# Attention and mixture-of-experts block on one Trainium2 core: value products, projections, transposes and filler units in another order on TensorE

## The chip, the core and the metric

The kernel runs on one core of one Trainium2 chip. The metric is device microseconds of one execution, from start to end. The engines are named as in the profile: PE (TensorE, matrix products; PEld is its weight loads), DVE (VectorE), ACT (ScalarE), POOL (GpSimd) and SP (SyncE, which issues most DMA transfers). Each has a queue of its own and works through it in order; they wait for each other by semaphores.

## The reference, cut to what matters

One sequence of 2048 tokens with 128 features goes through causal attention (16 heads of 64) and then a mixture of 8 experts (2 chosen for each token) with one shared expert. All is float32.

```python
x = x + attn(layernorm(x))            # 16 heads, D = 64, causal, softmax over keys
#   qkv    = x @ qkv_w + qkv_b
#   probs  = softmax(where(mask, q @ k.T / 8, -0.7 * float32_max))
#   result = (probs @ v) @ out_w + out_b
x = x + shared_ffn(layernorm(x)) + sum over the 2 best experts of weight * expert_ffn(layernorm(x))
#   ffn(x) = (silu(x @ gate.T) * (x @ up.T)) @ down.T      # 352 hidden features
```

## The kernel before, in words

**Steps.** The 16 heads are taken as 8 pairs j, the 2048 tokens as 16 blocks of 128, and the blocks of queries as 8 pairs m, each with the keys of blocks 0 to 2m+1. A step is one (j, m); there are 64. Within a pair the order of m is `turns = [2, 7, 0, 6, 1, 5, 3, 4]` (L393), so that a short step (m = 2, 0, 1, 3) and a long one (m = 7, 6, 5, 4) take turns. `at` is the place in the pair, 0 to 7; m=2 has `at` 0 and six key blocks.

**Scores.** `score_units` (L403) gives units that each compute one 512-wide piece of scores for both heads on PE (L438, form 64*128 of the array), which DVE scales, masks and copies out of PSUM with a row maximum (L449, L453). After the last piece of a row ACT takes the exponential (L470). The scores of a step are computed four steps ahead if it is long, two if it is short (`coming`, L701).

**Transposes.** The probabilities must be turned before the product with the values. Of a short step all blocks are turned on PE (`turn`, L532, matmul L538) and copied out of PSUM by ACT to `pT` (L541). Of a long step most blocks go another way: DVE transposes 32x32 squares (L512), and DMA moves them to DRAM and back (`stage`, L516, then `turned`, L530). The two or four blocks on and next to the diagonal, the tail, are turned on PE and copied by ACT to `tail` (`turn_last`, L543), two steps ahead.

**Values and projection.** `times_v` (L563) multiplies by the values (L570, form 128*64 of the array) and adds up in one of two PSUM buffers `av`. After the last block, `divide` (L589) multiplies by the inverse sums on DVE, which gives `aT`. `finish` (L672) calls `project` (L594): two products with the output weights on PE (L597, form 128*128) and one addition into the residual `xr` on DVE (L598). It is called one group after the division; until then the step stands in `ending`. In the last pair it also starts the routing of finished tokens (`route_units`, L214), whose units `route_on` (L664) runs one at a time.

**PSUM.** Scores, transposes, projections and q/k/v units take their PSUM tiles from one pool of six buffers in turn (`psp`, L161, tag "r"). A matmul that opens a tile waits until the tile six places back has been copied out by DVE or ACT.

**Filler.** `fill` holds the q, k and v units of the next pair (L361, L378); DVE copies out q (L371), ACT k (L373) and v (L385).

**Order.** For PE and DVE the order of the program is the order of the queue (`manual_schedule`, L630); on ACT, POOL and SP the framework's scheduler sets it. The loop over the steps (L681) runs two or three groups of each step. A long step (`near` is true) has three: the tail (k = 0), and two halves of the blocks that came by DMA (k = 1, 2). In each group the loop does, in this order: one filler unit (short steps), transposes that are due on DVE, the turns of the group's blocks on PE, `finish` of the step before if one stands in `ending`, the products with the values, `divide`, one filler unit (long steps), in a long step's k = 0 the tails of the step after next, in k = 1 the load of `turned`, and then three units of scores. In the second group of a long step PE therefore has the projection of the short step before, then the values of the first half:

```python
            if ending is not None:
                finish(*ending)
                ending = None
            ...
            for t in ready:
                jt, mt, b = t[:3]
                times_v(*t, qkv[jt][0][2])
```

**After attention** come the routing of the last tokens, a scatter of the tokens to their experts by POOL (L328), and the experts, whose results POOL scatters back (L991).

Of the kernel before, what the change touches and what calls it, by code (L numbers as in the profile page):

```python
# [23 lines left out]
def attention_then_moe(  # L24
# [58 lines left out]
    def load_wq(j, engine):  # L83
        wq_of[j] = norm.tile([P, 3, 2, D], F32, tag="wq", name=f"wq_{j}", bufs=3)
        engine.dma_start(wq_of[j], qkv_w[:, :, 2 * j : 2 * j + 2, :])
# [7 lines left out]
    with nc.allow_non_contiguous_dma(reason="1024 numbers"):  # L93
# [16 lines left out]
        fill=MASKED,  # L110
# [6 lines left out]
    for e in range(NE):  # L117
# [9 lines left out]
        fill=0.0,  # L127
# [226 lines left out]
    def qkv_units(j):  # L354
        kT = pool.tile([P, S], F32, tag="kT", name=f"kT_{j}")
        qT = [None] * NG
        vt = pool.tile([P, NT, P], F32, tag="vt", name=f"vt_{j}")

        def qk_unit(s, n):
            pq = psp.tile([P, 512], F32, tag="r", name=f"pq_{j}_{s}_{n}")  # L360
            nc.tensor.matmul(  # L361
                pq,
                wq_of[j][:, s, :, :],
                xnT[:, ts(n, 512)],
                start=True,
                stop=True,
            )
            bias = bqk[:, s, j : j + 1]
            if s == 0:
                qT[n] = pool.tile([P, 512], F32, tag=f"qT{n}", name=f"qT_{j}_{n}", bufs=1)  # L370
                nc.vector.tensor_scalar_add(qT[n], pq, bias)  # L371
            else:
                nc.scalar.activation(kT[:, ts(n, 512)], pq, AF.Identity, bias=bias)  # L373

        def v_unit(g):
            pv = psp.tile([P, 4, P], F32, tag="r", name=f"pv_{j}_{g}")
            for t in range(4):
                nc.tensor.matmul(  # L378
                    pv[:, t, :],
                    xnT[:, ts(4 * g + t, P)],  # L380
                    wq_of[j][:, 2, :, :],
                    start=True,
                    stop=True,
                )
            nc.scalar.copy(vt[:, ts(g, 4), :], pv)  # L385

        q, k = ([lambda s=s, n=n: qk_unit(s, n) for n in range(NG)] for s in range(2))
        return (kT, qT, vt), q, k, [lambda g=g: v_unit(g) for g in range(NG)]
# [10 lines left out]
    def by_slabs(m):  # L399

        return (2 * m) // 4 * 4 if 2 * m >= NT // 2 else 0
# [130 lines left out]
    def turn(j, m, b, dst):  # L532

        tr = psp.tile([P, 2, 256], F32, tag="r", name=f"tr_{j}_{m}_{b}")
        q0 = 1 if b == 2 * m + 1 else 0
        for h in range(2):
            for q in range(q0, 2):
                nc.tensor.transpose(  # L538
                    tr[:, h, ts(q, P)], rows_of[j, m][q][:, h, ts(b, P)], ident
                )  # L540
        nc.scalar.copy(dst[:, :, q0 * P :], tr[:, :, q0 * P :])  # L541

    def turn_last(j, m):  # L543

        tail_of[j, m] = pool.tile([P, 4, 2, 256], F32, tag="tail", name=f"tail_{j}_{m}", bufs=1)
        for b in range(by_slabs(m), 2 * m + 2):
            turn(j, m, b, tail_of[j, m][:, b - by_slabs(m)])
# [41 lines left out]
    def divide(j, m):  # L589
        aT = pool.tile([P, 256], F32, tag="aT", name=f"aT_{j}_{m}", bufs=1)  # L590
        nc.vector.tensor_mul(aT, av_of[j, m], inb_of[j, m])
        return aT

    def project(j, m, aT):  # L594
        po = psp.tile([P, 2, E], F32, tag="r", name=f"po_{j}_{m}")
        for q in range(2):
            nc.tensor.matmul(po[:, q, :], aT[:, ts(q, P)], wo[:, j, :], start=True, stop=True)  # L597
        nc.vector.tensor_add(xr[:, ts(m, 2), :], xr[:, ts(m, 2), :], po)  # L598
# [22 lines left out]
    steps = [(j, m) for j in range(NP) for m in turns]  # L621
# [21 lines left out]
    fill, later = deque(), deque()  # L643
    last = []
    ending = None
# [3 lines left out]
    def load_shared():  # L649
        for k, w in enumerate((w_gate, w_up, w_down)):  # L650
            t = norm.tile([P, 3 * P], F32, tag="wq", name=f"shared_{k}", bufs=3)
            if k < 2:
                t = t[:, :F]
                nc.sync.dma_start(t, w[:, NE, :])
            else:
                t = t.rearrange("p (c e) -> p c e", c=NFC)
                for c, (f0, fn) in enumerate(FCH):
                    nc.sync.dma_start(t[:fn, c, :], w[f0 : f0 + fn, NE, :])
            shared_w.append(t)
# [4 lines left out]
    def route_on():  # L664

        for units in routes:
            u = units.popleft()
            if u:
                u()
        routes[:] = [units for units in routes if units]  # L670

    def finish(j, m, aT):  # L672
        project(j, m, aT)
        if j == NP - 1:
            for number, batch in enumerate(batches):
                if m == batch[-1]:
                    assert len(routes) <= 1
                    blocks = [b for m in batch for b in (2 * m, 2 * m + 1)]
                    routes.append(deque(route_units(blocks, number)))

    for n, (j, m) in enumerate(steps):  # L681
        at = n % NM
        if at == 0 and j + 1 < NP:
            qkv[j + 1] = qkv_units(j + 1)


            _, q, k, v = qkv[j + 1]
            fill.extend([*k, *v, q[3]])
            later.extend([q[1], q[0], q[2]])
            if j + 2 < NP:  # L690
                load_wq(j + 2, nc.sync)
        if at == 0 and j == NP - 1:
            load_shared()
        if at == 5 and later:
            assert not fill
            fill.extend(later)
            later.clear()
        if at == 6 and j + 1 < NP:
            assert not fill
        near = by_slabs(m)  # L700
        coming = scores_of(n + (4 if near else 2))  # L701
        if n == 0:
            coming.extend(scores_of(3))

        if near:
            groups = [list(range(near, 2 * m + 2))]
            groups += [list(range(k, k + near // 2)) for k in range(0, near, near // 2)]

            runs = [3, 3, len(coming) - 6] if n > 1 else [0, 3, 3]
        else:  # L710
            groups = [list(range(k, min(k + 3, 2 * m + 2))) for k in range(0, 2 * m + 2, 3)]
            half = len(coming) // 2 if n else 6
            runs = {1: [len(coming)], 2: [2 * (half // 2), half], 3: [0, half, half]}[len(groups)]
        for k, group in enumerate(groups):
            for _ in range(1 if n else 3):
                if fill and not near:
                    fill.popleft()()
            if n == 2:
                turn_slabs(2, age=False)
            turn_slabs(1)  # L720
            now = [turned(j, m, b) for b in group]
            if k == 0:
                spread(j, m)
            if ending is not None:
                finish(*ending)
                ending = None
            if n >= len(steps) - 2 and (n < len(steps) - 1 or k < 2):
                route_on()
            ready, last = (last + now, []) if near else (last, now)
            for t in ready:  # L730
                jt, mt, b = t[:3]
                times_v(*t, qkv[jt][0][2])
                if b == (by_slabs(mt) or 2 * mt + 2) - 1:
                    assert ending is None
                    ending = (jt, mt, divide(jt, mt))
            if n < len(steps) - 2:
                route_on()

            for _ in range(1 if n > 1 or k == 2 else 2):
                if fill and near:  # L740
                    fill.popleft()()
            if n < 2 and k == 1 - n:
                turn_slabs(2, age=False)
            turn_slabs(1, age=False, due=True)
            if n >= len(steps) - 2:
                route_on()
            if near and k == 0 and n + 2 < len(steps):
                turn_last(*steps[n + 2])
            if n == 0 and k == 0:
                turn_last(*steps[1])  # L750
                load_turned(*steps[1])
            if near and k == 1 and n + 2 < len(steps):
                load_turned(*steps[n + 2])
            for _ in range(runs[k] if k < len(groups) - 1 else len(coming)):
                if coming:
                    coming.popleft()()
            if len(steps) - 4 <= n < len(steps) - 2:
                route_on()
# [328 lines left out]
```

## Time and profile before

| | us |
|---|---|
| median of 3 runs | 1003.43 (1003.37 to 1006.6) |
| profiled execution | 1008.16, its span 1006.3 |
| PE busy | 943.7 (94%) |
| DVE busy | 749.7 (75%) |
| ACT busy | 540.9 (54%) |
| POOL busy | 204.9 (20%) |
| one head pair in the steady part, 400.40 to 500.64 | 100.24, of which PE is busy 98.09 |

In lines of the profile the columns of an instruction in order of time are: start in us from the span's start, busy us, engine, line of the kernel, operation, output <- input, shape, count, and in brackets how long the engine stood before it and what ended that wait. Rows of the same kind that follow each other are merged. In a table by stretch of time the columns are: stretch, its length, busy us and count of PE, PEld, DVE, ACT and POOL, the granted clock of PE (1.00 is full), the DMA engines' share and GB/s. In a list of waits they are: us in total, times, longest. Matmuls are pipelined and their ends are modelled, so an idle PEld does not mean that PE stands. A busy share is a mean over stages with different limits.

### The profile page before, as it was taken

How to read it: one execution, taken by the hardware profiler on the slowest of the kernel's cores; microseconds unless marked ns; L12 is line 12 of the kernel's file. 1: busy time of each engine (PE TensorE's matmuls, PEld its weight loads, DVE VectorE, ACT ScalarE, POOL GpSimd, SP SyncE). 2: the span in 40 equal slices, each digit the busy share in tenths (PEclk: the TensorE clock that was granted, in tenths of full speed). 3: DMA queues.
4: the chain of work that ended last, by engine and by line, in shares of the span. 5: the costliest groups of instructions: out<-in, count | busy, mean ns of one | idle time of the engine just before them, and what ended most of it. 6: DMA issues, size and time to landing. Idle time of an engine off the chain costs nothing. (4 is left out here: it accounts for less than half of the span.)

```text
span 1006.3 us, 18409 instructions
## 1 busy us (share of the span) xinstructions
PE 943.7 (94%) x5930; PEld 567.9 (56%) x5930; DVE 749.7 (75%) x2359; ACT 540.9 (54%) x1017; POOL 204.9 (20%) x393
## 2 busy tenths in 40 slices
PE   4998899999999999999999999999999898989996
PEld 1464555565556555655565556555655455657774
DVE  3786788778877877787778777877788886755554
ACT  4573556555655565556555655565466553425552
POOL 2040111111111111111111111111211103634441
PEclk9998999999999999999999999999999997999998
DMA  9568648864896488748874887588648864723104
GB/s 329 173 203 288 198 149 267 261 220 155 261 276 206 155 260 265 216 157 261 270 210 157 260 266 210 164 256 270 209 150 274 268 193 146 216 61 85 40 24 132
DMA packets 112670, 205.31 MB, mean 204 GB/s; under 512 B 16864, under 2 KB 104258, under 8 KB 107456
## 3 DMA queue, kind: packets, MB, share of 16 engines
q1 hardware_dynamic: 102816, 190.65, 59.4%
q0 software_dynamic: 8032, 13.22, 5.5%
q8 instruction: 48, 0.79, 0.3%
q10 hardware_dynamic: 1728, 0.27, 0.2%
q14 instruction: 46, 0.38, 0.1%
HBM read 105.10 MB, written 99.35 MB: 203 GB/s over the span
## 5 line engine op out<-in xcount | busy, mean ns | idle before, releaser
L470 ACT ACTIVATE row<-row,neg 128x1920 f32<-128x1920 f32 (+15 forms) x256 | 306.2, 1202 | 198.7 <-DVE neg L467 87.3
L438 PE MATMUL sc<-kT,qT 64*128 64x512 f32 (+3 forms) x1280 | 298.0, 552 | 11.3 <-ACT tail L541 5.2
L449 DVE TENSOR_SCALAR_CACHE_REDUCE row<-sc 128x512 f32<-128x512 f32 x384 | 243.3, 685 | 76.4 <-PE sc L438 65.8
L438 PEld LDWEIGHTS sc<-kT,qT 64*128 64x128 f32 x1280 | 123.9, 186 | 152.5 <-issue 83.6
L512 DVE STREAM_TRANSPOSE row<-row 128x1024 f32<-128x1024 f32 (+1 forms) x128 | 190.3, 1491 | 5.1 <-ACT row L470 5.1
L570 PE MATMUL av<-turned,vt 128*64 128x256 f32 x1280 | 158.3, 395 | 2.1 <-DMA turned<-stage 2.1
L453 DVE CUSTOM_DVE_ANT_0 row<-sc,mask 128x384 f32<-128x384 f32 (+3 forms) x256 | 114.9, 486 | 18.2 <-PE sc L438 17.6
L538 PE MATMUL tr<-ident,row 128*128 128x128 f32 x896 | 121.4, 281 | 6.5 <-DVE row L449 2.1
L538 PEld LDWEIGHTS tr<-ident,row 128*128 128x128 f32 x896 | 102.2, 144 | 41.1 <-issue 19.4
L570 PEld LDWEIGHTS av<-turned,vt 128*64 128x64 f32 x1280 | 88.5, 140 | 64.9 <-issue 23.5
L501 POOL DMA_DIRECT2D invd<-inv x60 | 43.1, 718 | 392.1 <-DVE inv L499 285.1
L541 ACT COPY pT<-tr 128x512 f32<-128x512 f32 (+1 forms) x160 | 78.6, 553 | 77.6 <-PE tr L538 77.2
L583 POOL DMA_DIRECT2D inb<-invd x120 | 71.6, 602 | 187.8 <-DMA invd<-inv 112.7
L570 PE MATMUL av<-pT,vt 128*64 128x256 f32 (+1 forms) x640 | 79.6, 371 | 6.3 <-ACT pT L541 5.9
L361 PE MATMUL pq<-xnT,wq 128*128 128x512 f32 x128 | 71.3, 647 | 0.1
L570 PEld LDWEIGHTS av<-pT,vt 128*64 128x64 f32 x640 | 38.5, 136 | 46.9 <-ACT pT L541 18.8
L541 ACT COPY tail<-tr 128x512 f32<-128x512 f32 x96 | 43.9, 520 | 15.1 <-PE tr L538 15.1
L991 POOL DMA_INDIRECT ybuf<-yo,to x39 | 38.3, 982 | 61.3 <-ACT yo L990 61.3
L371 DVE TENSOR_SCALAR qT<-pq,bqk 128x512 f32<-128x512 f32 x32 | 23.9, 747 | 34.6 <-PE pq L361 34.6
L470 ACT ACTIVATION_READ_ACCUMULATOR row<-row,neg 128x1 f32 x256 | 49.6, 194 | 0.0
L597 PE MATMUL po<-wo,aT 128*128 128x128 f32 x256 | 43.7, 294 | 5.7 <-DVE rest L280 2.5
L597 PEld LDWEIGHTS po<-wo,aT 128*128 128x128 f32 x256 | 34.0, 193 | 22.9 <-DVE row L449 16.3
(170 smaller groups left out, 894.8 us busy)
## 6 DMA issues: line engine op xcount, KB each, us to landing
stage<-row SPq DMA_DIRECT2D x256, 192.0 KB, 3.7
turned<-stage SPq DMA_DIRECT2D x16, 3072.0 KB, 11.1
stage<-row SPq DMA_DIRECT2D x256, 128.0 KB, 2.7
turned<-stage SPq DMA_DIRECT2D x16, 2048.0 KB, 8.7
zbuf<-zeros SPq DMA_DIRECT2D x8, 1056.0 KB, 11.4
inb<-invd POOLq DMA_DIRECT2D x120, 64.0 KB, 3.2
zs<-zbuf SPq DMA_DIRECT2D x39, 66.0 KB, 1.8
yt<-ybuf SPq DMA_DIRECT2D x4, 512.0 KB, 4.2
```

What stands on the lines that cost most here:

```text
L361: nc.tensor.matmul(pq, wq_of[j][:, s, :, :], xnT[:, ts(n, 512)], start=True, stop=True,)
L438: nc.tensor.matmul(sc[:, :cw], qT[i // 4][hd, ts(i % 4, P)], keys, start=True, stop=True)
L449: nc.vector.tensor_scalar(dst, src, SCALE, None, ALU.mult, ALU.max, accum_out=mh)
L453: nc.vector.tensor_tensor_reduce(out=rows[:, h, c0 : c0 + cw], in0=scs[h][:, :cw], in1=mask[:, 512 - cw : 512], scale=SCALE, scalar=-F32_M ...
L470: nc.scalar.activation(row, row, AF.Exp, bias=neg[:, h : h + 1], accum_out=sums[:, h : h + 1])
L501: small_dma(j, m)(invd_of[j, m].rearrange("n (a i) -> a n i", a=4), inv,)
L512: nc.vector.transpose(row, row)
L538: nc.tensor.transpose(tr[:, h, ts(q, P)], rows_of[j, m][q][:, h, ts(b, P)], ident)
L541: nc.scalar.copy(dst[:, :, q0 * P :], tr[:, :, q0 * P :])
L570: nc.tensor.matmul(av_of[j, m][hd, q0 * P :], vt[:, b, hd], pT[:, h], start=(b == near), stop=(b == (near or 2 * m + 2) - 1),)
L583: small_dma(j, m)(inb[h * D : (h + 1) * D, :].rearrange("d (q p) -> d q p", q=2), row.partition_broadcast(D),)
L597: nc.tensor.matmul(po[:, q, :], aT[:, ts(q, P)], wo[:, j, :], start=True, stop=True)
```

## The change

No instruction is added or taken away. The loop over the steps is edited in three places.

1. In a long step's second group (`near and k == 1`), `finish` is called behind the products with the values, not ahead of them. The projection's two matmuls come behind the first half's 8 or 12 blocks of values for both heads; then come the filler unit, if there is one, and the scores.
2. In a long step's first group, `turn_last` for the step after next is called ahead of the filler unit, not behind it. Step n = 1 keeps the old place.
3. In the second group of the six-block step (m = 2, `at` 0, from the second pair on), the filler unit comes behind the turns of the group's blocks and the projection, and ahead of the values; before, it came ahead of the turns.

In the built program DVE's order differs in one place: in the last pair, the addition of one projection (m = 3) into `xr` (L598) stands behind the routing's choice of the second expert instead of inside it. POOL's and SP's orders are the same. On ACT the copies follow: in m = 7's step the tail's copies stand ahead of a key copy, and the next key copy stands ahead of row 10's exponentials; in m = 6's the tail's copies stand ahead of a value copy; in m = 5's the first of the two tail copies stands ahead of row 7's exponentials, the second behind them, as before; in m = 2's a key copy stands behind the `pT` copies.

```diff
         for k, group in enumerate(groups):
             for _ in range(1 if n else 3):
-                if fill and not near:
+                if fill and not near and (at or not k or not n):
                     fill.popleft()()
...
             if k == 0:
                 spread(j, m)
-            if ending is not None:
+            values_first = near and k == 1
+            if ending is not None and not values_first:
                 finish(*ending)
                 ending = None
             if n >= len(steps) - 2 and (n < len(steps) - 1 or k < 2):
                 route_on()
+            if n and not at and k and fill:
+                fill.popleft()()
             ready, last = (last + now, []) if near else (last, now)
             for t in ready:
                 ...
                     ending = (jt, mt, divide(jt, mt))
+            if ending is not None and values_first:
+                finish(*ending)
+                ending = None
             if n < len(steps) - 2:
                 route_on()
+            if n > 1 and near and k == 0 and n + 2 < len(steps):
+                turn_last(*steps[n + 2])
 
             for _ in range(1 if n > 1 or k == 2 else 2):
                 if fill and near:
                     fill.popleft()()
...
-            if near and k == 0 and n + 2 < len(steps):
+            if n == 1 and k == 0:
                 turn_last(*steps[n + 2])
```

## The prediction, made before the changed kernel ran

> **What bounds the kernel now.** I read the page first, then the busy time of one head pair, then TensorE in order of time, and last the chain of waits at the end.
>
> ```profile
> span 1006.3 us, 18409 instructions
> PE 943.7 (94%) x5930; PEld 567.9 (56%) x5930; DVE 749.7 (75%) x2359; ACT 540.9 (54%) x1017; POOL 204.9 (20%) x393
> ```
>
> ```profile
> 400.40:500.64 100.24, 98.09 (x640) 56.40 (x640) 80.22 (x237) 57.87 (x106) 16.11 (x32) 1.00 0.72 225
> 832.30:845.80 13.50, 12.81 (x57) 8.81 (x58) 7.50 (x47) 2.52 (x8) 2.89 (x3) 0.50 0.60 206
> ```
>
> One head pair (eight steps) takes 100.24 us and repeats to the hundredth; PE is busy for 98.09 of it, DVE for 80.22, ACT for 57.87. So in the steady part only a few us a pair can be won, and only from PE. The second stretch is at the end of attention: PE ran at half its clock (the column that reads 0.50).
>
> The list of waits would have it that the projection is a place where PE stands:
>
> ```profile
> PEld po L597 <- DVE row L449: 16.3, 22, 1.5
> ```
>
> In order of time this is not so. The weight load idles while PE still streams scores:
>
> ```profile
> 405.53 2.21 PE L438 MATMUL sc<-kT,qT 64*128 64x512 f32 x12
> 407.67 0.71 PE L597 MATMUL po<-wo,aT 128*128 128x128 f32 x4
> 408.31 2.81 PE L570 MATMUL av<-turned,vt 128*64 128x256 f32 x24
> ...
> 427.36 1.13 PE L361 MATMUL pq<-xnT,wq 128*128 128x512 f32 x2
> 428.32 0.82 PE L538 MATMUL tr<-ident,row 128*128 128x128 f32 x6
> 429.07 2.59 PE L438 MATMUL sc<-kT,qT 64*128 64x512 f32 x8
> 432.27 1.40 PE L438 MATMUL sc<-kT,qT 64*128 64x512 f32 x4 [0.62 <-ACT tail L541]
> 433.60 0.71 PE L597 MATMUL po<-wo,aT 128*128 128x128 f32 x4
> ...
> 472.02 0.61 PE L597 MATMUL po<-wo,aT 128*128 128x128 f32 x4
> 472.46 1.02 PE L361 MATMUL pq<-xnT,wq 128*128 128x512 f32 x2
> 473.33 1.25 PE L538 MATMUL tr<-ident,row 128*128 128x128 f32 x10
> ```
>
> The reader is to see two things. First, the stall of a pair in step m=5: scores start at 429.07 and wait until 432.27 for ACT's copy of the tail, which stands in ACT's queue behind two exponentials:
>
> ```profile
> 429.38 1.15 ACT L470 ACTIVATE row<-row,neg 128x1024 f32<-128x1024 f32 x1 [3.02 <-DVE neg L467]
> 430.53 1.13 ACT L470 ACTIVATE row<-row,neg 128x1024 f32<-128x1024 f32 x1
> 431.66 0.83 ACT L541 COPY tail<-tr 128x512 f32<-128x512 f32 x2
> ```
>
> Second, a change of array form (the 64*128 of scores, the 128*64 of values, the 128*128 of the rest) costs PE time: the projection takes 0.64 between scores and values (407.67 to 408.31), but 0.44 between two 128*128 neighbours (472.02 to 472.46).
>
> At the end the chain goes through PE:
>
> ```profile
> 829.38 1.06 PE L260 MATMUL pr<-gwT,xnT 128*128 128x8 f32 x8
> 832.99 1.19 PE L597 MATMUL po<-wo,aT 128*128 128x128 f32 x4 [2.55 <-DVE rest L280]
> 834.11 3.68 PE L570 MATMUL av<-turned,vt 128*64 128x256 f32 x16
> 837.72 0.65 PE L301 MATMUL rk<-hot,below 128*128 128x40 f32 x2
> 839.96 3.68 PE L570 MATMUL av<-turned,vt 128*64 128x256 f32 x16
> ```
>
> The projection stands for 2.55 us behind DVE's routing, and the values behind it, which need nothing of that, take 3.68 instead of the 1.95 of the same row at 462.36.
>
> **The change part by part.** It adds and removes no instruction. POOL and SP keep their order, every DMA with them; DVE moves one addition, in the last pair; ACT follows PE's new order in copies.
>
> *Values ahead of the projection (long steps, second group).* In steady steps no wait goes, since none was there; what goes is a change of form where a 128*128 unit follows the values. Before: projection 0.64, then the q/k unit 1.05 (488.73 to 489.78), 1.69 together. After: the projection loses its way out (0.10) and the unit its way in (0.10; 0.96 at 427.36 against 0.87 at 472.46): 0.20 less. This holds for m=7, 6, 5 of pairs 1 to 6 and m=7, 5 of pair 0: 20 x 0.20 = -4.0. In m=4 scores follow, and three changes stay three: 0. In the first long step the values wait 2.1 for their transfer (78.88); the projection, 0.6, ran inside that wait and now comes behind it: +0.6. DVE's addition into xr waits for the later projection, and DVE's queue stands meanwhile. Behind it are q copies and evictions of scores that come after the projection on PE anyway, and DVE idled there 2.6, 2.55, 1.9 and 1.3 us (m=7, 6, 5, 4) against a delay of about 2.7, 2.7, 1.9 and 1.2 us: 0, with bounds of 0 and +0.4 for m=4, where it is closest. The values start 0.64 earlier; their transfers land some 7.5 to 11 us after issue, issued 18 us or more ahead (490.29 for 508.54): 0.
>
> *Tails' turns ahead of the filler.* In m=5 the turns run at 427.36, ACT idles from 426.4 and copies the first tail at once; the second copy (0.40) stays behind the exponentials, which DVE sets, and ends at about 432.05. The sixth score matrix alone now waits for it, and runs alone: 1.05 as in m=4 (460.67 to 461.72), so scores end at 433.2, not 433.60: -0.40 in seven pairs = -2.8. Bounds: 0 if the order on ACT costs as much again, -1.9 if the stall went whole. In m=7 and m=6 nothing stalled: 0. ACT now has the last key projection of m=7 ahead of row 10's exponentials, which end at about 493.3, not 490.6; DVE needs them at 495.76: 0, covered by 2.5 us.
>
> *A unit between turns and values (six-block step).* The values wait 0.98 for ACT's second copy at 475.52, behind row 13's exponentials. PE has the same work ahead of that point in either order: 0, bounds -0.1 and +0.1 a pair.
>
> *The last pair.* In m=6 the projection begins 1.02 after the last score matmul (806.06 to 807.08), against 0.20 in an earlier pair (407.46 to 407.67): -0.8. In m=7 it stood 0.9, but evictions then wait for staging transfers until 790.33: 0. In m=4 DVE's addition leaves the routing's chain: -0.3. In m=5 the first values run in the 2.55 us gap, at full clock 1.95; ranks then start at 834.4 (DVE's hot ends at 834.3) instead of 837.72, second values end at 837.6, and the next projection is free when DVE's chain reaches it at 840.1, not 846.70: -6.6 if the half clock goes with the gap. If it stays, ranks still start 3 us earlier: -3.0.
>
> [...] The rows first: the granted clock is 1.00 up to 832.2, 0.50 from 832.3 to 845.8 and 1.00 from 846.0, and the gap of 2.55 ends at 832.99. [...]
>
> **Sum.** -4.0 + 0.6 - 2.8 - 0.8 - 0.3 - 6.6 = -13.9, or -10.3 with the half clock kept. The profiled execution took 1008.16 us (span 1006.30, 1.86 around it), so 994.3; it lies 4.73 above the median, 1003.43. Half-clocked stretches may be part of that excess, so that the median has less of the last term to lose. From the median: 989.5 to 993.1. I take 991.
>
> **Rivals.** (1) The half clock stays or moves: 1003.43 - 10.3 = 993. For it: it lasted over 13.5 us though PE worked after 833. Against: another half-clocked stretch (0.50 from 801.6 to 804.8) also follows a gap of about 2 us, which ends at 801.49. [...] (2) The steady gain reappears as waits for evictions: DVE is busy 14.76 of the 15.49 us from 417.35 to 432.84. Then 6.2 of the sum goes and 4.1 to 7.7 stay: 996 to 999. Against: each such stretch begins with DVE idle for PE. (3) Slower: row 10's exponentials, 2.6 us late on ACT, make DVE's transposition and the staging behind it late. It decides once the delay passes the 2.5 us of cover; paid whole in seven pairs it is 18, less 10: 1011. Against: the cover is measured, and repeats. (4) Nothing is gained anywhere, as the projection wasn't waited for: 1003; against it speaks the 2.55 us gap.
>
> **How the numbers follow.** Forecast 0.52; half clock kept 0.20; (2) 0.16; (3) 0.06; (4) 0.06. 0.5% of 1003.43 is 5.0 us, about what a measurement of this kernel can tell from no change. Faster: 0.52 + 0.20 + half of (2), 0.08 = 0.80; same: 0.08 + 0.06 = 0.14; slower 0.06. The range reaches from the forecast with the tail stall gone whole (991 less 5) to the upper end of (2), 999.
>
> **What would show it.** A pair takes 99.2 us instead of 100.24; PE's wait for the tail's copy stays, on one score matrix; the projection follows the values at the same pitch; the slices at 832 lose their half clock, and row 10's exponentials start near 490.3 in that pair. I am wrong if the pair is longer, or if a longer wait for turned, vt or pT appears.

## The result, and the profile after

The changed kernel takes 993.31 us (median of 4 runs, 991.6 to 995.36), beside 1003.4 for the kernel before in the same comparison: a ratio of 0.9891, 95% interval 0.9867 to 0.9915. Its profiled execution took 992.08 us. The forecast was 991, the range 986 to 999.

The head of the page after (each engine's count is as before; the 6 records more are semaphore waits on PE):

```profile
span 990.2 us, 18415 instructions
PE 932.6 (94%) x5930; PEld 557.8 (56%) x5930; DVE 752.7 (76%) x2359; ACT 541.0 (55%) x1017; POOL 205.0 (21%) x393
```

One head pair, and a stretch at the end of attention that answers to the half-clocked one of before (columns as in the table by stretch of time: stretch, length, busy us and count of PE, PEld, DVE, ACT, POOL, granted clock, DMA share, GB/s):

```profile
396.58:495.60 99.02, 97.32 (x641) 55.67 (x640) 80.63 (x237) 57.94 (x105) 16.13 (x32) 1.00 0.73 227
...
828.00:841.00 13.00, 11.40 (x95) 8.31 (x96) 8.61 (x55) 5.67 (x15) 9.95 (x11) 1.00 0.47 172
```

A pair takes 99.02 us instead of 100.24, again to the hundredth in the steady part. PE's busy time in it falls by 0.77, its idle time by 0.45, so the gain is partly shorter work and partly a shorter stall. The granted clock is 1.00 all through that end stretch.

TensorE in order of time, after; step m=6, then m=5:

```profile
400.60 2.21 PE L438 MATMUL sc<-kT,qT 64*128 64x512 f32 x12
402.74 2.81 PE L570 MATMUL av<-turned,vt 128*64 128x256 f32 x24
405.48 0.71 PE L597 MATMUL po<-wo,aT 128*128 128x128 f32 x4
406.03 1.06 PE L378 MATMUL pv<-wq,xnT 128*128 128x128 f32 x8
407.02 2.42 PE L438 MATMUL sc<-kT,qT 64*128 64x512 f32 x12
...
422.31 0.88 PE L538 MATMUL tr<-ident,row 128*128 128x128 f32 x6
423.02 1.02 PE L361 MATMUL pq<-xnT,wq 128*128 128x512 f32 x2
423.97 2.84 PE L438 MATMUL sc<-kT,qT 64*128 64x512 f32 x10
426.98 1.12 PE L438 MATMUL sc<-kT,qT 64*128 64x512 f32 x2 [0.17 <-ACT tail L541]
```

The projection now takes 0.55 (405.48 to 406.03) instead of 0.64, and the v unit behind it 0.99 (406.03 to 407.02) instead of 1.09. In m=5 five of the six score matrices run through, and the sixth alone waits for ACT's second tail copy. ACT, around the same place:

```profile
423.05 0.58 ACT L541 COPY tail<-tr 128x512 f32<-128x512 f32 x1 [1.78 <-PE tr L538]
424.30 1.15 ACT L470 ACTIVATE row<-row,neg 128x1024 f32<-128x1024 f32 x1 [0.66 <-DVE neg L467]
...
425.45 1.13 ACT L470 ACTIVATE row<-row,neg 128x1024 f32<-128x1024 f32 x1
...
426.58 0.35 ACT L541 COPY tail<-tr 128x256 f32<-128x256 f32 x1
```

One copy stands ahead of row 7's exponentials, the other behind them. In the list of waits, the row that seemed to accuse the projection has shrunk from 16.3 to 0.8, and DVE's wait for the projection has grown from 18.8 to 51.7:

```profile
DVE xr L598 <- PE po L597: 51.7, 43, 6.9
...
PEld po L597 <- DVE row L449: 0.8, 2, 0.4
```

Neither number is a gain or a loss in itself: in e8 below the first row stays as long and the pair gets shorter, and e1, whose list has 52.4 for the second, has no longer step in its steady pairs. TensorE at the end of attention, in order of time:

```profile
819.36 1.95 PE L570 MATMUL av<-turned,vt 128*64 128x256 f32 x16
821.98 0.68 PE L597 MATMUL po<-wo,aT 128*128 128x128 f32 x4 [0.67 <-DVE rest L280]
823.42 0.39 PE L301 MATMUL rk<-hot,below 128*128 128x40 f32 x2 [0.76 <-DVE inv L496]
823.63 1.04 PE L309 MATMUL rk<-hot,ones 128*128 128x32 f32 x8
824.60 1.95 PE L570 MATMUL av<-turned,vt 128*64 128x256 f32 x16
```

The values run while DVE routes; the projection's wait is 0.67, where it was 2.55, and both halves of the values take 1.95, where they took 3.68.

Where the time went, by comparing the start of each step's first value product in the two traces: 1.87 us of the difference lie ahead of anything that the change touches (the start of the kernel); pair 0 gains 0.23; pairs 1 to 6 gain 1.22 each; the last pair gains 0.76 in m=7, 0.82 in m=6, 5.79 in m=5, 0.44 in the step after it and 0.25 in m=4; 1.4 are given back in the experts' part, behind the last projection.

### The profile page after: what moved, and what is told of

It is laid out like the page before. It is cut to its first block, busy times and chain, and to the rows that moved or that the text cites. A ratio compares the mean times of both kernels' runs of the same rounds, so it can differ in the third digit from the quotient of the medians.

```text
span 990.2 us, 18415 instructions
## 1 busy us (share of the span) xinstructions
PE 932.6 (94%) x5930; PEld 557.8 (56%) x5930; DVE 752.7 (76%) x2359; ACT 541.0 (55%) x1017; POOL 205.0 (21%) x393
## 5 line engine op out<-in xcount | busy, mean ns | idle before, releaser
L570 PE MATMUL av<-turned,vt 128*64 128x256 f32 x1280 | 154.8, 389 | 2.1 <-DMA turned<-stage 2.1
L538 PEld LDWEIGHTS tr<-ident,row 128*128 128x128 f32 x896 | 98.0, 141 | 34.5 <-DVE row L449 13.4
L361 PE MATMUL pq<-xnT,wq 128*128 128x512 f32 x128 | 67.6, 618 | 0.1
L598 DVE TENSOR_TENSOR xr<-xr,po 128x256 f32<-128x256 f32 x64 | 26.7, 418 | 52.5 <-PE po L597 51.7
L373 ACT ACTIVATE kT<-pq,bqk 128x512 f32<-128x512 f32 x32 | 21.9, 695 | 52.4 <-PE pq L361 52.4
L970 DVE TENSOR_TENSOR hk<-sk,uk 128x352 f32<-128x352 f32 x39 | 20.3, 520 | 36.1 <-PE uk L966 36.1
```

The lines of the kernel that those rows point to most:

```text
L361: nc.tensor.matmul(pq, wq_of[j][:, s, :, :], xnT[:, ts(n, 512)], start=True, stop=True,)
L538: nc.tensor.transpose(tr[:, h, ts(q, P)], rows_of[j, m][q][:, h, ts(b, P)], ident)
L570: nc.tensor.matmul(av_of[j, m][hd, q0 * P :], vt[:, b, hd], pT[:, h], start=(b == near), stop=(b == (near or 2 * m + 2) - 1),)
```

## The experiments

They ran on three chips: e1 to e4 on one, c_before, e5, e6 and e7 on a second, c_after, e8 and e9 on a third. On all three the kernel before takes about 1020 us (medians 1020.91, 1020.17 and 1019.89 in the three comparisons), 16 to 18 more than in the comparison above; "the first chip" is the one of that comparison. Ratios are always against the kernel before on the same chip. What is compared is above all the length of a steady pair, which repeats to 0.02 in nearly every trace, and the length of each step in it, both counted from one first value product to another.

**e1: values ahead of the projection, alone.**

```diff
-            if ending is not None:
+            values_first = near and k == 1
+            if ending is not None and not values_first:
                 finish(*ending)
                 ending = None
...
+            if ending is not None and values_first:
+                finish(*ending)
+                ending = None
```

> The kernel before with part 1 alone (projection behind the values in every long step's second group). Theory A (each long step with a filler unit behind the values saves one change of array form, 0.20; nothing waited): a steady pair goes from 100.24 to 99.64 (m=7, 6 and 5 shorter by 0.20 each, m=4 by 0); the last pair loses what it lost in the changed kernel, about 8 (m=7 0.76, m=6 0.82, m=5 about 5.8, the rest later); the time falls by 20 x 0.20 + 8 = 12, less the 1.4 that the changed kernel gave back at its end: 10.6. Theory B (the steady gain of the changed kernel is all from the tails and the unit, by their new places in ACT's queue): the pair stays 100.24 and only the last pair gains, about 7.

Measured: 1013.98 us, ratio 0.9935 (0.9911 to 0.996). A pair takes 99.70: m=7 is shorter by 0.19, m=6 by 0.13, m=5 by 0.22, m=4 by 0. In the last pair m=6 gains 0.82 and the step with m=5's values 5.12, both against the first chip's trace. The steady half of theory A holds, to 0.06 us a pair (99.64 was expected; m=6 gave less than 0.20, and why is not shown). The whole time fell by 6.6 (by the ratio), not by 10.6: against c_before below, the trace of the kernel before on a chip of like time, m=5 gains 1.37, not 5.12, and m=7 is 0.65 longer.

**e2: the same in the last pair alone.**

```diff
+            values_first = near and k == 1 and j == NP - 1
```

> The kernel before with part 1 in the last pair alone. Theory A (the last pair's gain comes from the projection's wait for routing, which the values no longer share): pairs 1 to 6 stay at 100.24, the last pair is shorter by about 8, the 2.55 us gap ahead of the projection at 832.99 and the half clock after it are gone; the time falls by 6.5 to 8. Theory B (the half clock has another cause, for instance the load before it, and went away in the changed kernel only because the time had shifted): the half clock stays near 832 and the last pair gains 3 to 4.

Measured: 1017.34 us, ratio 0.9968 (0.9952 to 0.9983); pairs stay at 100.24. The projection's gap shrinks as in the changed kernel (a wait of 0.67), but a half-clocked stretch of 3.41 us comes all the same, one value group later. TensorE in order of time:

```profile
832.57 0.68 PE L597 MATMUL po<-wo,aT 128*128 128x128 f32 x4 [0.67 <-DVE rest L280]
834.01 0.39 PE L301 MATMUL rk<-hot,below 128*128 128x40 f32 x2 [0.76 <-DVE inv L496]
...
835.20 3.59 PE L570 MATMUL av<-turned,vt 128*64 128x256 f32 x16
```

The second half of the values, at 835.20, takes 3.59 instead of 1.95. The gain of 3.3 us (by the ratio) is half of what theory A expected, and with the half clock still there both signs of theory B came; e5 shows below that the gap is a cause all the same. The values' move does not exclude the half clock here. The two waits of 0.67 and 0.76 are left, in every trace of this order, and the traces differ in how they fall into the stretches of 3.41 us on whose borders the granted clock changed (832.25 and 845.90 in the kernel before on the first chip, four stretches apart). In e2, just ahead of the half clock:

```profile
831.91:835.33 3.42, 2.00 (x16) 1.85 (x18) 3.07 (x20) 1.55 (x5) 0.00 (x0) 1.00 0.37 105
```

And the same place in the changed kernel on the first chip:

```profile
819.59:823.00 3.41, 2.40 (x20) 1.38 (x16) 3.07 (x18) 2.56 (x6) 0.00 (x0) 1.00 0.69 169
823.00:826.42 3.42, 3.00 (x26) 2.25 (x26) 3.05 (x22) 0.00 (x0) 0.00 (x0) 1.00 0.54 120
```

In e2 both waits lie within one stretch, as in e1, e6 and e9, and half clock follows in all four. In the changed kernel a border cuts the second wait (first chip) or lies between the two (c_after), and it does not follow; in e7 a border cuts the first, and it follows all the same.

**e3: the tails' turns ahead of the filler, alone.**

```diff
+            if n > 1 and near and k == 0 and n + 2 < len(steps):
+                turn_last(*steps[n + 2])
...
-            if near and k == 0 and n + 2 < len(steps):
+            if n == 1 and k == 0:
                 turn_last(*steps[n + 2])
```

> The kernel before with part 2 alone (tails' turns ahead of the filler unit). Theory A (in m=5 one of two waiting score matrices is freed earlier): a pair goes from 100.24 to about 99.75 (the changed kernel gained 0.71 in m=5, 0.20 of it assigned to the values); the longest wait for the tail's copy moves from the fifth score matrix to the sixth and stays about as long; the last pair's gap of 2.55 us and its half clock stay; the time falls by 7 x 0.5 = 3.5. Theory B (part 2 gains only together with part 1, as the filler unit that it lets through first would meet the projection): the pair stays within 0.1 of 100.24.

Measured: 1015.96 us, ratio 0.9951 (0.9929 to 0.9974). A pair takes 99.67: m=5 gains 0.48, m=7 and m=6 0.04 to 0.05 each. The gap of 2.55 in the last pair is still there, and half clock follows it (from 832.00), though for 3.41 us and not for 13.65. Theory A holds. One pair takes 100.37, which no theory foresaw.

**e4: the unit of the six-block step, alone.**

```diff
-                if fill and not near:
+                if fill and not near and (at or not k or not n):
                     fill.popleft()()
...
+            if n and not at and k and fill:
+                fill.popleft()()
```

> The kernel before with part 3 alone (in the six-block step the filler unit between turns and values). Theory A (PE has the same work ahead of the values' wait for ACT's second copy, only the wait is shorter because the unit fills it): the pair is 0.09 shorter, as the changed kernel's m=2 was, 100.15; the time falls by 0.6, which is less than the runs can tell. Theory B (the 0.09 was a follow-up of part 2 or part 1): the pair stays 100.24.

Measured: 1017.87 us, ratio 0.9963 (0.9942 to 0.9984). The pair is 100.15, all of the 0.09 in m=2. The wait of the values for ACT's second copy is 0.98 as before; what is shorter is the next group of scores (1.18 before, 1.09 here), ahead of which ACT now finishes its `pT` copies without the key copy between them. The three parts alone give 0.54 + 0.57 + 0.09 = 1.20 a pair; together they gave 1.22, so the parts add up. The whole time fell by 3.8 (by the ratio, interval 1.6 to 5.9) where theory A expected 0.6. No trace shows the rest: the profiled execution took 1020.10, 2 us more than c_before's.

**c_before: the kernel before on the chip of e5, e6 and e7.**

> The kernel before itself, to have its trace from the chip on which the next three run. Both theories: steady pairs of 100.24. Theory A (the median of 1020.9 of the second chip against 1003.4 of the first comes from the last step of attention, where ACT stands between copies while POOL scatters, as in the runs of parts 1, 2 and 3 alone): on the slow chip that step shows a wait of PE of 6 to 12 us at its transposes (L252), against 0.95. Theory B (it is spread over the kernel): the pair is longer than 100.24.

Measured: 1018.05 us, pairs of 100.24 but for one of 100.46. The last step but one of attention, from m=3's first value product to m=4's, is 14.4 us longer than on the first chip. TensorE at its transposes:

```profile
853.14 1.63 PE L252 MATMUL pt<-ident,row 128*128 128x128 f32 x4 [8.67 <-ACT row L197]
```

ACT in the same stretch, in order of time:

```profile
852.12 0.59 ACT L541 COPY pT<-tr 128x512 f32<-128x512 f32 x1 [2.98 <-remote]
...
861.42 0.65 ACT L254 COPY xnT<-pt 128x256 f32<-128x256 f32 x2 [7.18 <-remote]
```

ACT stands between copies whose input PE has long finished, released by something that isn't in the trace, while POOL issues its scatter. Theory A holds on where most of the time is; why ACT stands is open. POOL's scatter alone is not the reason: on the first chip POOL scatters at the same place (from 842.30), and ACT's waits there are 1.7 and less, but for one at 844.72 that PE ends.

**e5: the 2.55 us gap filled with three products.**

```diff
+            if n == len(steps) - 3 and k == 1:
+                spare = psp.tile([P, 512], F32, tag="r", name="spare")
+                for _ in range(3):
+                    nc.tensor.matmul(spare, ident, xnT[:, :512], start=True, stop=True)
```

> The kernel before with three products of 128*128x512 ahead of the projection at the 2.55 us gap of the last pair; their result is never read. Theory A (a window of 3.41 us in which PE is busy for less than about half is followed by half clock; the gap leaves that window at 0.47): with the gap filled no half-clocked stretch begins within 6 us of it, the values behind it take 1.95 instead of 3.0 to 3.7, and the projection begins no later. The time falls by 2 to 4. [...]

Measured: 1018.67 us, ratio 0.9985 (0.9961 to 1.001). The table by stretches of 3.41 us, the kernel before on the first chip:

```profile
828.84:832.25 3.41, 1.60 (x14) 1.36 (x12) 3.24 (x14) 1.96 (x5) 0.00 (x0) 1.00 0.83 202
832.25:835.67 3.42, 2.68 (x12) 1.92 (x14) 3.09 (x20) 1.63 (x5) 0.00 (x0) 0.50 0.41 113
835.67:839.08 3.41, 3.41 (x17) 2.09 (x15) 0.72 (x6) 0.00 (x0) 0.00 (x0) 0.50 0.88 274
```

The same table for c_before, on the chip of e5:

```profile
827.43:830.84 3.41, 0.86 (x8) 0.80 (x8) 3.20 (x17) 2.42 (x6) 0.00 (x0) 1.00 0.84 219
830.84:834.25 3.41, 3.41 (x16) 2.17 (x18) 3.00 (x20) 0.78 (x3) 0.00 (x0) 0.50 0.42 90
834.25:837.67 3.42, 3.42 (x32) 2.39 (x28) 1.33 (x9) 0.00 (x0) 0.00 (x0) 1.00 0.86 316
```

And for e5, the gap filled:

```profile
826.70:830.10 3.40, 3.40 (x14) 1.84 (x14) 3.16 (x18) 2.40 (x6) 0.00 (x0) 1.00 0.82 210
830.10:833.51 3.41, 3.41 (x30) 2.47 (x28) 2.93 (x19) 0.69 (x3) 0.00 (x0) 1.00 0.48 99
```

Behind a window with PE busy for 1.60 or 0.86 of 3.41 us, the next ran at half clock (0.50); with the gap filled, 3.40 of 3.40, it did not (1.00), and the values take 1.95. All five traces that have the gap (before, c_before, e3, e4 and e8) show half clock behind it. Counted from the products ahead of the gap (L260), the ranks (L301) start 1.70 earlier than in c_before, 6.03 instead of 7.73 behind them, although PE did more. So the gap is the cause here, though its 2.55 us are shorter than the window's 3.41. The whole time, which theory A put 2 to 4 lower, is lower by 1.5 with an interval around zero: the step gains the 1.70, the next step keeps it to 0.04, and the part behind that is 1.24 longer in this trace, which is no more than it varies by from trace to trace.

**e6: the changed kernel with the projection behind the second group's scores** (all pairs but the last).

```diff
-            if ending is not None and values_first:
+            if ending is not None and values_first and j == NP - 1:
                 finish(*ending)
                 ending = None
...
             for _ in range(runs[k] if k < len(groups) - 1 else len(coming)):
                 if coming:
                     coming.popleft()()
+            if ending is not None and values_first:
+                finish(*ending)
+                ending = None
```

> The changed kernel, but outside the last pair the projection is moved on behind the scores of the second group, so that it stands between scores and values again. Theory A (the values' move saves a change of array form and no wait): m=7, 6 and 5 get back their 0.19, 0.13 and 0.22, m=4 nothing, a pair takes 99.02 + 0.54 = 99.56, and the time rises by 7 x 0.54 = 3.8 against the changed kernel. Theory B (the values gain by no longer standing behind the projection's wait): the pair stays 99.02.

Measured: 1033.86 us, ratio 1.0133 (1.0074 to 1.0193); a pair takes 102.53, 3.5 longer than with the change. Both theories miss it. Most of the extra is no change of form: at the turn from m=4 to the next pair's m=2 (2.4 to 2.8 longer) the framework placed row 13's exponentials ahead of all of m=2's `pT` copies, where in the changed kernel one copy goes first, and PE stands for them. TensorE there:

```profile
487.62 1.30 PE L361 MATMUL pq<-xnT,wq 128*128 128x512 f32 x2 [2.15 <-ACT pT L541]
```

ACT runs two exponentials of 1.8 us each from 483.44 and starts its copies at 487.00. The half clock then follows in every pair, 3.41 us each (a granted clock of 0.98 over the pair from 411.79). m=7, on the other hand, got shorter by 1.39: the scores ahead of its end take 1.72 (512.58 to 514.30) where the changed kernel's take 3.31 (492.29 to 495.60), as a weight load that stood for 1.32 there no longer stands. Another sequence of PSUM buffers may be the reason; no run shows it. The run doesn't tell the theories apart; e8 does.

**e7: the changed kernel with two score units, not three, in the first group of m=5 and m=4.**

```diff
-            runs = [3, 3, len(coming) - 6] if n > 1 else [0, 3, 3]
+            runs = [3 if len(coming) < 8 else 2, 3, len(coming) - 6] if n > 1 else [0, 3, 3]
```

> The changed kernel with two score units instead of three in the first group of m=5 and m=4, and one more in the last group, so that the sixth score matrix of that group, which waits 1.1 to 1.3 for the copy of the last tail, comes later. Theory A (that wait is the only thing that PE stands for there): a pair gets shorter by up to 2.2 and the time by up to 7 x 2.2 = 15; as the scores' rows end later, ACT's exponentials and the transfers of turned blocks start later by some 2, which have 7 or more to spare. Theory B (the wait comes back at another matmul, since DVE and ACT set the pace there: DVE is busy for 14.8 of 15.5): a pair gains less than 0.5 or gets longer.

Measured: 992.06 us, ratio 0.9723 (0.966 to 0.9786), although the step that was longer in c_before is longer here too, by 7.8 against the first chip. A pair, in the table by stretch of time:

```profile
391.85:488.67 96.82, 95.21 (x642) 54.95 (x641) 80.37 (x237) 58.03 (x105) 16.19 (x32) 1.00 0.78 236
```

TensorE at the score groups that had waited, m=5 and m=4:

```profile
419.24 1.99 PE L438 MATMUL sc<-kT,qT 64*128 64x512 f32 x8
421.16 1.95 PE L570 MATMUL av<-turned,vt 128*64 128x256 f32 x16
...
446.16 1.99 PE L438 MATMUL sc<-kT,qT 64*128 64x512 f32 x8
448.08 1.95 PE L570 MATMUL av<-turned,vt 128*64 128x256 f32 x16
```

Eight score matmuls now run through in 1.99 in both steps, and the values follow at once. 96.82 is 2.20 below the changed kernel: 1.29 from m=5 and 1.00 from m=4, less 0.09 in m=2. Theory A holds whole in the pair: PE stood for nothing else there. Six pairs of 2.20 are 13.2 us; the ratios of e7 and c_after lie some 18 us apart, and the rest is in the first and last steps, which differ between traces. The sixth score matrix's wait for the tail, which the change only shortened, is gone once other work comes first.

**c_after: the changed kernel on the chip of e8 and e9.**

> The changed kernel itself, beside the next two on one chip. Both theories: a steady pair of 99.02. Theory A (what costs the second chip its 16 us is ACT standing between copies in the last step while POOL scatters, and the change touches nothing of that): the wait of PE at L252 in the last step is 6 to 12 us here too, and on such a chip the time is 1003 to 1008, 10 to 17 below the kernel before; on a chip like the first it is 993.

Measured: 1010.4 us, ratio 0.9896 (0.9855 to 0.9938), the same ratio as on the first chip. The pair is 99.02. The last step but one stands at other places than in c_before (PE for 3.73 at L252 and 6.71 at L260, ACT for 10.67 ahead of its copy at L254), so the place was half wrong, and the time came out 2 above the range expected.

**e8: the kernel before, with the filler unit moved up to the projection, the values still behind it.**

```diff
+            early = near and k == 1 and n > 1
+            if early and fill:
+                fill.popleft()()
             ready, last = (last + now, []) if near else (last, now)
...
-                if fill and near:
+                if fill and near and not early:
                     fill.popleft()()
```

> The kernel before, with the values left behind the projection; instead the filler unit of a long step's second group (m=7, 6, 5) is put ahead of the values, directly behind the projection. Theory A (what the move of the values saves in a steady pair is a change of array form, because projection and filler unit then stand side by side): the pair is shorter by the same 0.19 + 0.13 + 0.22 = 0.54, so 99.70, and m=4, which has no filler unit there, by 0. Theory B (it is the values' earlier start that counts): the pair is 100.24 or longer, since the values now start 1 later. In the last pair nothing changes in either, so the time falls by 7 x 0.54 = 3.8 or by nothing.

Measured: 1015.37 us, ratio 0.9965 (0.9939 to 0.999). A pair, in the table by stretch of time:

```profile
398.00:497.66 99.66, 97.52 (x641) 56.02 (x640) 80.13 (x237) 57.97 (x106) 16.12 (x32) 1.00 0.72 226
```

TensorE in m=6, in order of time:

```profile
404.76 0.71 PE L597 MATMUL po<-wo,aT 128*128 128x128 f32 x4
405.31 1.06 PE L378 MATMUL pv<-wq,xnT 128*128 128x128 f32 x8
406.29 2.81 PE L570 MATMUL av<-turned,vt 128*64 128x256 f32 x24
409.04 2.42 PE L438 MATMUL sc<-kT,qT 64*128 64x512 f32 x12
```

The row of the list of waits that had named the projection:

```profile
PEld po L597 <- DVE row L449: 17.9, 23, 2.3
```

The pair gets shorter by 0.58, 0.19 to 0.20 in each of m=7, m=6 and m=5 and nothing in m=4, although the values start about 1 us later and the wait listed for the projection is as long as ever (16.3 before). Projection, unit and values take 4.28 (404.76 to 409.04) in place of 4.47 (407.67 to 412.14). Theory B is out: what the values' move is worth in a steady pair is one change of array form in each long step that has a filler unit.

**e9: e7, with the projection behind the scores in m=7 alone.**

```diff
-            if ending is not None and values_first:
+            if ending is not None and values_first and (m != 7 or j == NP - 1):
...
+            if ending is not None and values_first:
+                finish(*ending)
+                ending = None
```

> The kernel with two score units in the first group (e7_two), and in m=7 of all pairs but the last the projection moved on behind the second group's scores, as in e6_late. Theory A (in e6_late that move took the 1.61 us wait at the short row's score matrix away, at 494.55 in the changed kernel, by another sequence of PSUM buffers, and its losses came from m=6, 5 and 4): the pair goes from 96.83 to about 95.4, the time falls by 7 x 1.4 = 10 against e7_two. Theory B (the sequence of buffers or ACT's order moves the wait elsewhere, as it did in e6_late's m=4): the pair stays or gets longer by up to 2.

Measured: 989.58 us, ratio 0.9705 (0.9675 to 0.9734), which the runs can't tell from e7. Counted between the first value products of m=0, pairs now vary from 96.16 to 97.48, on average 96.86; what varies is m=7, and the next step makes up for it, since counted between those of m=5 they take 96.71 to 96.80, where e7's take 96.81 to 96.90. m=7 is shorter by up to 1.39, but m=5 (and most times m=6) loses about 0.65: the first eight score matmuls of m=5 take 2.63 where e7's took 1.99, as TensorE's order of time shows:

```profile
417.43 2.63 PE L438 MATMUL sc<-kT,qT 64*128 64x512 f32 x8
```

Theory B holds: the wait moved, and the pair is shorter by 0.1 at most.

## Why the prediction was right, and where not

**Values ahead of the projection: right, by the mechanism given.** 0.20 each in m=7, m=6 and m=5 and 0 in m=4 was the estimate; e1 measured 0.19, 0.13, 0.22 and 0, and e8 gave 0.19 to 0.20 three times over with the values left where they were. The reading that the listed wait is none, because PE streams scores meanwhile, is shown by e8. The traces price a way in or out at about 0.1 us (from before to after, the projection in m=6 goes from 0.64 to 0.55 and the v unit behind it from 1.09 to 0.99); by what a change of form costs time, they can't show. DVE's addition, which now waits for the later projection, cost nothing, as said: its wait grew by 33 us in total and no steady step shows it. The +0.6 in the first long step is not settled: m=7 of pair 0 got 0.10 shorter in the first chip's trace and is 0.48 longer in c_after than in c_before, but e5, whose edit doesn't touch it, has it 3.97 shorter than the first chip's kernel before.

**Tails' turns: right, somewhat too small.** The stall stays on the sixth score matrix alone. The term was 0.40; e3 measured 0.48 in m=5 and another 0.09 in m=7 and m=6 together, which were costed at 0 though the sequence of units there changed too. It holds for six pairs, not seven: in pair 0 the stall is as it was, 0.70 on the fifth matrix in both kernels. Row 10's exponentials run from 484.38 to 487.3 in the changed kernel, and DVE starts on them at 489.67: 2.4 of cover are left over, as the prediction's 2.5 (493.3 to 495.76). That figure is what remains behind the delay; rival (3), which sets the delay of 2.6 against it, counts the delay twice, so its condition was set too near. It did not come, nor did rival (2): no new wait of the size of the gain appears in a steady pair.

**The unit: a gain of 0.09, not 0,** near the end of its bounds, -0.1. The wait at ACT's copy stayed at 0.98 as argued; the gain was one group further on, which the prediction did not price.

**The last pair: the gap was read rightly, but that the half clock went is in part luck.** m=6 gave 0.82 (0.8). In m=7 the 0 rested on the evictions' wait for transfers: on the first chip 0.76 was gained; from c_before to c_after, two chips of like time, 0.94 was lost. There the first projection's wait (0.48) is gone too, but the second projection, which had none, now waits 1.46. So the wait moves, as said, but not by an equal amount. m=4's 0.25 is near its 0.3, without a run that separates it. m=5 was put at 6.6 with the half clock gone, and 5.79 was measured at that step. e5 shows that the gap of 2.55 causes the half clock. But the change leaves two short waits in its place, and of the seven traces with this order five have half clock there (e1, e2, e6, e7 and e9); the two of the changed kernel are those without. And one kernel has the stretches of 3.41 us at different places of its work: in the kernel before, a border lies 2.87 behind the start of the products ahead of the gap (829.38) on the first chip, and 3.72 behind it (827.12) in c_before.

Nor was 6.6 the worth of that term in the usual execution. 3.75 of the 5.79 go with the length of the half-clocked stretch of before: the same kernel in c_before has 3.41 us of it instead of 13.65, and from c_before to c_after m=5 gains 2.04 (1.4 in e1 and e2, where half clock stays). That is the term that was mis-sized against the median: the profiled execution of before lay 4.73 above its median, and I let only a part of that count. With 2.0 instead of 6.6 and the steady part as measured, 6 x 1.22 + 0.2 + 0.8 + 2.0 = 10.3, and the medians differ by 10.1. What this sum leaves out (0.76, 0.44 and 0.25 gained, 1.4 given back) is 0.05 in all in the profiled executions. That the other executions of before on the first chip had the short stretch is argued from this agreement; they left no trace.

So 991 was close by two errors of opposite sign: the steady part 1.3 too small (6.2 against 7.5), the last pair too large. Rival (1) gave 993, the number measured, but for a reason that the trace of after does not bear out: there the half clock behind the gap went.

**What the half clock goes with.** The prediction left open whether it goes with the gap of 2.55 us. e5 decides it here: with the gap filled, the half clock behind it is gone, so an idle time of 2.55 us was enough. What fits the traces is PE's busy share in a stretch of 3.41 us, on the grid of the granted clock: 0.47 and 0.25 ahead of the half clock in the two traces of the kernel before, 1.00 in e5, where none follows. The "about half" in theory A of e5 was the author's estimate: in the traces before and after, 0.45 to 0.49 was followed by half clock and 0.52 to 0.55 was not, but in e2 0.59 was.

## What to carry to other kernels

- A row in the list of waits can name an engine that streams other work meanwhile; in e8 the wait listed for the projection was 17.9 us in total (16.3 before) while the pair got 0.58 shorter. Look at the order of time before a move is made for such a row.
- Put products of the same array form side by side: here each change of form saved is worth about 0.19 us (e8).
- When a copy is late because it stands behind an engine's long instructions, giving TensorE other ready work first was worth more (2.2 us a pair, on top of the change) than starting the copy's producer earlier (0.57).

## What the runs showed of the hardware

- **The granted clock changed on a grid of 3.41 us.** In the thirteen traces, the half-clocked stretches begin on a grid of 3.41 us and last one to four windows of it (3.41 us in c_before, 13.65 in the kernel before on the first chip). PE's busy share in a window, worked out from the matmul records, goes with what follows. Of the full-clock windows from 30 us on in the traces before and after, 6 of 6 with under 0.40 busy are followed by half clock, 4 of 7 between 0.40 and 0.65, and 0 of 536 above 0.65; in all thirteen traces, 56 of 56, 36 of 78 and 2 of 3438. The gap of 2.55 us was followed by half clock in all five traces that have it, and in e2 so were two waits of 0.67 and 0.76 in one window (PE busy for 2.00 of 3.42). What ends the stretch is not settled: in the kernel before it lasted four windows on the first chip, with PE busy throughout the last three, and one window in c_before.
- **One kernel took 16 to 18 us more on three chips than on the first, and one place stands out.** The pairs agree to the hundredth (but for one of 100.46); c_before's trace is 14.4 longer than the first chip's in the last step but one of attention, where ACT stands for 2 to 11 us at a time while POOL scatters. This was not tried further.
- **A move of two matmuls can cost elsewhere.** In e6 a pair got 3.5 us longer than with the change: 2.4 to 2.8 of it at the turn to m=2, where ACT's exponentials came ahead of the copies that PE waits for, with 1.39 gained in m=7 and 2.3 lost in m=6, m=5 and m=3. Other moves stayed where they were made: e4's 0.09 is in m=2 alone.
